# Layer 1's first convolution split twice and moved behind the projection, in a two-layer attention kernel

## The chip, the cores and the metric

The kernel runs on one core of one Trainium2 chip. The metric is the device time of one execution, in microseconds (us); the time of a kernel is the median of its runs. TensorE does the matrix products, VectorE (DVE) the two-input elementwise work, ScalarE (ACT) exponentials, copies and biases, GpSimd (POOL) a share of the elementwise work, and SyncE (SP) issues most of the transfers. Each engine executes its own queue in order.

## The reference

Eight images of 512 channels and 1024 pixels (32 x 32) in fp32 go through two attention layers. Cut to what matters:

```
# layer 0: 8 heads of 64 channels
h = group_norm(x, 32 groups)
q, k, v = split(w_qkv @ h + b_qkv)
weight = softmax(q_head^T k_head / 8)            # 1024 x 1024 for each head
x = x + w_proj @ (weight applied to v) + b_proj
# layer 1: one head of 512 channels
xn = group_norm(x, 8 groups)
q, k, v = q_w @ xn + q_b, k_w @ xn + k_b, v_w @ xn + v_b
attn = softmax(q^T k / sqrt(512))
x = x + p_w @ (attn applied to v) + p_b
```

## The kernel before

**Products merged ahead of time.** For layer 1 the kernel never forms q, k and v. It multiplies the weights once, in the prologue: m from the weights of q and k, and z from those of v and p. Then per image g = m h + ubias (the "first convolution" of the title, named g), scores = h^T g, and the values are read straight from z h.

**One level of Strassen.** Every large product goes through `wino` (L227): both factors are cut in two by two, and seven products take the place of eight. A product is a `step` (L240), 8 records of 128x512 on TensorE for a convolution. The sums of parts that it needs are made ahead of it: for weights by `left_sums` (L151), for images by `right_sums` (L165), eight subtractions of 128x512 (`image_factors`, L340). The order of steps is 1, then `middle`, then 4 and 3. The last two are not issued at once but laid in `tail`, and the next stage's `wino` issues them after its own step 1 (`finish`, L223), so that there is always a product between a stage's end and its readers. PSUM pools a, b and c have two buffers each; step 2 adds into the bank of step 1 after a copy of it (`t`, L249) has been taken, and steps 6, 7 and 4 share a bank.

**Two levels.** Layer 0's k and q of images 1 to 7 are split once more by `conv2` (L416): 49 products of 256 columns, in pairs `(1, 5), (2, 6), (7,), (3, 4)`. They need *inner factors* (L400), 28 subtractions of 128x256 on GpSimd per image, and twice-split weights that the prologue makes on GpSimd and writes to DRAM (`keep2`, L296, four operations of 128x896 and seven transfers). VectorE adds the products up (L439), GpSimd does the additions for the lone pair (`more`, L444), and four activations on ScalarE put the bias on, half a channel tile at a time (`biased_half`, L451).

**Order of the stages.** TensorE's instructions are pinned in program order (`matmul`, L66); the other engines' instructions are ordered by the framework unless they are pinned too (`tc.keep_in_program_order`). Small work is laid in `background`, from which each step takes a few, or in `hooks` of a stage's steps. The loop at L928 runs for each image b:

- layer 0's attention of image b (`attention0`, L577): 8 blocks (4 head pairs `hp`, 2 halves `tb`), each with 32 score products, exponentials of 128x1024 on ScalarE (L594), their running sum on VectorE (L596, L598), 32 products with v, and then the sums over keys on TensorE and the reciprocals (`reciprocals`, L548). The reciprocals go through DRAM (`rows`, `r`) to be spread over partitions; GpSimd multiplies the block by r (L615), and for the last block VectorE does (`scaled`, L617). Work for other stages goes in 16 slots, `extra`, two per block: group norm's application for layer 1 of image b-1 (`apply`, L140, ScalarE) stands in slots 3, 5, 7 and 9
- for b > 0, g of image b-1 (`layer1_scores`, L892), one-level, then the projection of image b (`projection`, L838) with its residual additions (L845, L847) and statistics (L98, L103), then layer 1's scores (`scores1`, L623: part 0 and part 1), z and values (`values1`, L672) of image b-1. Group norm's two small products for image b (`gmean`, `gvar`) stand in hooks of the scores' part 0
- v, k and q of image b+1 (`values`, `keys_and_queries`).

Weights come from DRAM through three buffers of 4 x 7 x 512 bytes per partition each (`wpool`), in the order of the list `uses` (L310 to L314), one `load_weight` (L317) per use. The prologue (L752) makes m, the factors of q, k and v, and image 0's v, q and k; the factors of p, m and z are made in image 0's attention (`later`, L797).

Of the kernel before, what the change touches and what calls it, by code (L numbers as in the profile page):

```python
# [29 lines left out]
def two_attention_blocks_kernel(  # L30
# [145 lines left out]
    def main_path(ctx):  # L176
# [117 lines left out]
        wdram2 = {n: dram.tile([P, 7, 7, P], F32, name=f"sums2_{n}") for n in "qk"}  # L294

        def keep2(n, t):  # L296

            u = wpool.tile([P, 4, 7, P], F32, tag="w", name=f"prepare2_{n}")
            quarter = lambda k, i: t[:, :, k, ts(i, P)]
            a11, a21, a12, a22 = quarter(0, 0), quarter(0, 1), quarter(1, 0), quarter(1, 1)  # L300
            s1, s2, s3, s4 = (u[:, i, :, :] for i in range(4))
            for dst, x, y, op in (
                (s1, a21, a22, ALU.add), (s2, s1, a11, ALU.subtract), (s3, a11, a21, ALU.subtract),
                (s4, a12, s2, ALU.subtract),
            ):
                nc.gpsimd.tensor_tensor(dst, x, y, op)
            for j, f in enumerate((a11, a12, s4, a22, s1, s2, s3)):
                nc.sync.dma_start(wdram2[n][:, :, j, :], f)

        twice = [("k", 0), ("k", 1), ("q", 0), ("q", 1)]  # L310
        uses = ["v", "p", *twice] if B > 1 else ["p"]
        for b in range(1, B):
            uses += ["m", "p", "z"] + (["v", *twice] if b + 1 < B else [])
# [3 lines left out]
        def load_weight():  # L317
            if uses:
                n = uses.pop(0)
                t = wpool.tile([P, 7 * C], F32, tag="w", name=f"w_{n[0]}_{len(uses)}")  # L320
                if n in twice:
                    t = t.rearrange("p (i j m) -> p i j m", i=4, j=7)
                    i = n[1]
                    t = t[:, : 4 - i]
                    nc.sync.dma_start(t, wdram2[n[0]][:, 4 * i : 4 + 3 * i])
                else:
                    t = t.rearrange("p (i k m) -> p i k m", i=7, k=2)
                    nc.sync.dma_start(t, wdram[n])
                loaded.append((n, t))
# [10 lines left out]
        def image_factors(h, uid):  # L340

            tiles = [pair_tile(f"t{i}_{uid}") for i in (1, 2, 4)]
            halves = lambda t: (t[:, :HT], t[:, HT:])
            return right_sums(
                [halves(t) for t in h[:2]], [halves(t) for t in h[2:]],
                [lambda j, t=t: t[:, j, :] for t in tiles], nc.vector.tensor_sub,
            )
# [52 lines left out]
        def inner_factors(hf, uid):  # L400

            f, steps = {}, []
            for p in ORDER:
                t = big_tile(f"inner{p}_{uid}", (P, 4, 2 * P))
                t1, t2, t3, t4 = (t[:, i, :] for i in range(4))
                b11, b12, b21, b22 = (hf[p][k][:, ts(i, 2 * P)] for k in range(2) for i in range(2))
                f[p] = {1: b11, 2: b21, 3: b22, 4: t4, 5: t1, 6: t2, 7: t3}

                def make(ops=((t1, b12, b11), (t2, b22, t1), (t3, b22, b12), (t4, b21, t2))):
                    for dst, x, y in ops:  # L410
                        nc.gpsimd.tensor_tensor(dst, x, y, ALU.subtract)

                steps.append(make)
            return f, steps

        def conv2(n, f, bias, name, hooks=(), late=None):  # L416
# [123 lines left out]
            last = [lambda: biased_half(0, 1), lambda: biased_half(1, 0)]  # L540
# [3 lines left out]
            pair(3, (3, 4), [(0, 1), (1, 0)], [(0, 1), (1, 0)], [load_weight, *last])  # L544
# [3 lines left out]
        def reciprocals(total, uid, across):  # L548
# [14 lines left out]
            nc.sync.dma_start(rows.rearrange("j i n -> i j n"), rc[0:P:32, :, :])  # L563
            if across:
                r = pair_tile(f"r_{uid}")
                for j in range(2):
                    row = rows[j : j + 1].rearrange("j i n -> j (i n)")
                    nc.sync.dma_start(r[:, j, :], row.to_broadcast([P, HT]))
            else:
                r = rpool.tile([P, HT], F32, tag="r", name=f"r_{uid}")  # L570
                for j in range(2):
                    row = rows[j : j + 1].rearrange("j i n -> j (i n)")
                    nc.sync.dma_start(r[ts(j, 64), :], row.to_broadcast([64, HT]))
# [3 lines left out]
        def attention0(b, q, k, v, extra):  # L577
            a = channel_tiles(f"a0_{b}")
            n = 0
            for hp in range(KC):  # L580
                for tb in range(2):
# [31 lines left out]
                    r = reciprocals(total, uid, False)  # L613
                    if (hp, tb) != (KC - 1, 1):
                        nc.gpsimd.tensor_tensor(dst, dst, r, ALU.mult)  # L615
                    else:
                        scaled = lambda dst=dst, r=r: nc.vector.tensor_mul(dst, dst, r)  # L617

            assert not extra
            return a, scaled  # L620


        def scores1(b, gf, hf, uid, hooks):  # L623
# [7 lines left out]
            def part(j):  # L631
# [34 lines left out]
                wino(f"sc_{uid}_{j}", mm, done, middle=(6, 2, 5, 7) if j else (2, 5, 6, 7), hooks=() if j else hooks)  # L666
# [85 lines left out]
        def prologue():  # L752
# [35 lines left out]
            k = conv(weight_factors(first["k"][0]), hf, pcols("bk0"), "k0_0")  # L788
            finish()
            keep2("k", first["k"][0])  # L790
# [7 lines left out]
            for n in "pmz":  # L798
                t, steps = prepare(n)
                later.append(steps)  # L800
                later.append([lambda n=n, t=t: keep(n, t), load_weight])
# [3 lines left out]
                lambda: tc.keep_in_program_order(nc.vector.tensor_add(obias[0], bias[2], pcols("bp0"))),  # L805
            ])
# [27 lines left out]
        def attention_steps(a, scaled, b):  # L834
            af, steps = image_factors(a, f"a_{b}")
            return af, [[], [scaled, lambda: background.extend(steps)]]

        def projection(b, af, xt):  # L838

            norm = GroupNorm(1, f"1_{b}")  # L840

            def residual(i, r, c, ps, u):
                oc = 2 * r + i
                xh = xt[oc][:, ts(c, HT)]
                nc.vector.scalar_tensor_tensor(xh, ps, obias[0][:, oc : oc + 1], xh, ALU.add, ALU.add)  # L845
                if u is not None:
                    nc.vector.tensor_add(xh, xh, u)  # L847
                background.append(lambda: norm.half_stats(oc, c, xh))

                if c == 1 - r:  # L850
                    background.append(lambda: norm.end_stats(oc))
# [6 lines left out]
            by_channel(weight("p"), af, f"p_{b}", residual, after=[load_weight, store])  # L858
            return norm

        def norm_hooks(norm, uid):
            return [
                [], [], [all_background], [lambda: norm.group_mean(acc_tile(f"gmean_{uid}")[:, :KC])],
# [3 lines left out]
        def values(b, h, hooks=()):  # L867

            hf, steps = image_factors(h, f"h0_{b}")
            background.extend(steps)  # L870
# [21 lines left out]
        def layer1_scores(b, h, hooks):  # L892
            hf, steps = image_factors(h, f"h1_{b}")
            background.extend(steps)
            g = conv(
                weight("m"), hf, ubias, f"g1_{b}", middle=(2, 5, 6, 7), hooks=hooks, back=4,
                after=[load_weight, lambda: background.extend(gsteps)],
            )
# [6 lines left out]
            return hf, gf  # L905

        def layer1_rest(b, hf, gf, hooks, ahead):
            e, total, ef = scores1(b, gf, hf, f"1_{b}", hooks)
            state = {}

            def sums():
# [3 lines left out]
                weight("z"), hf, f"z1_{b}", hooks=[[], [], [], [], [sums]], back=3,  # L915
# [12 lines left out]
        for b in range(B):  # L928
# [11 lines left out]
            for i, f in enumerate(applies):  # L940
                extra[2 * i + 3].append(f)
            if b > 0:
                extra[0] += late
            psum_pools(f"attention_{b}", 1)
            a, scaled = attention0(b, q, k, v, extra)
            psum_pools(f"products_{b}", 2)
            xt = [load_x(b, c, "x") for c in range(KC)]
            af, ends = attention_steps(a, scaled, b)
            if b > 0:
                hf, gf = layer1_scores(b - 1, h, ends)  # L950
                norm1 = projection(b, af, xt)
# [5 lines left out]
                layer1_rest(b - 1, hf, gf, norm_hooks(norm1, f"1_{b}"), ahead)  # L957
                if b + 1 < B:
                    v, f, norm0 = values(b + 1, h)
                    q, k, late = keys_and_queries(b + 1, f, norm0, ())  # L960
            elif B > 1:
                v, f, norm0 = values(1, h, ends)
                norm1 = projection(0, af, xt)
                q, k, late = keys_and_queries(1, f, norm0, norm_hooks(norm1, "1_0")[1:])
            else:
                for f in sum(ends, []):
                    f()
                all_background()
                norm1 = projection(0, af, xt)
                finish()  # L970
                for f in sum(norm_hooks(norm1, "1_0"), []):
# [4 lines left out]
        hf, gf = layer1_scores(B - 1, h, ())  # L976
        layer1_rest(B - 1, hf, gf, (), ())
# [196 lines left out]
```

## Time and profile before

| what | value |
|---|---|
| median of three runs | 2906.97 us (2901.96 to 2907.82) |
| profiled execution, its own time | 2902.66 us |
| its span | 2900.9 us |
| TensorE busy | 2886.5 us |
| VectorE busy | 1932.5 us |
| ScalarE busy | 872.2 us |
| GpSimd busy | 468.9 us |
| transfers | 267.97 MB, 92 GB/s on the mean |

How to read it: the profile is one execution, followed by the hardware. The page's first part gives each engine's busy time, its share of the span and its instructions. A timeline line has the start and duration of a run of like instructions in us, engine, line, operation, output<-inputs by the program's names, shape and count; in brackets is the idle time before it and who ended it. Ends of TensorE's products are modelled, so two lines overlap a little; distances of starts are the better measure. TensorE's lines all carry the line of the helper `matmul` (L67); the names of the tiles tell the stage (`psa_g`: pool a, stage g). An fp32 product is two records. A waits line says engine, what waited, what it waited for, total us, times, and the longest.

### The profile page before, as it was taken

The page shows a single profiled execution, that of the slowest core. Times are in us where ns is not written, and L with a number is a line of the kernel's source. Part 1 is how long each engine was busy: PE and PEld are TensorE (multiplying, and loading weights), DVE is VectorE, ACT ScalarE, POOL GpSimd, SP SyncE. Part 2 cuts the span into 40 slices and gives each one's busy share as a digit, 9 for nine tenths or more (in the row PEclk, how much of TensorE's full clock was granted, in tenths as well). Part 3 has the DMA queues.
Part 4 walks back from the last instruction along what each step waited for, and adds up shares of the span by engine and source line. Part 5 has one row for each costly group of instructions (what it writes and reads, how often), then busy time and mean ns, then how long its engine had stood idle before and what let it go on. Part 6 is the DMA issues. An engine that isn't in the chain of part 4 may idle for free.

```text
span 2900.9 us, 29024 instructions
## 1 busy us (share of the span) xinstructions
PE 2886.5 (100%) x10838; PEld 1500.3 (52%) x10838; DVE 1932.5 (67%) x2613; ACT 872.2 (30%) x1117; POOL 468.9 (16%) x525
## 2 busy tenths in 40 slices
PE   9999999999999999999999999999999999999999
PEld 5435634565345653457434574346733458334544
DVE  5488687567766578665776557866577665776555
ACT  1251451214512055121551115411163112631110
POOL 3023210032200321003210122102121031110000
PEclk9999999999999999999999999999999999999999
DMA  8433403123122231222212232122411224011201
GB/s 277 153 137 109 159 19 110 72 103 132 34 98 92 95 113 48 84 92 105 107 48 80 92 135 77 48 80 99 154 55 44 80 103 151 26 59 65 94 1 66
DMA packets 84186, 267.97 MB, mean 92 GB/s; under 512 B 10371, under 2 KB 29891, under 8 KB 75974
## 3 DMA queue, kind: packets, MB, share of 16 engines
q1 hardware_dynamic: 83622, 265.89, 25.5%
q8 instruction: 87, 1.43, 0.2%
q14 instruction: 61, 0.50, 0.1%
q10 hardware_dynamic: 416, 0.16, 0.0%
HBM read 216.30 MB, written 49.72 MB: 92 GB/s over the span
## 4 chain that ended last, share of the span: by engine, by line
PE 98%; issue 1%; DVE 0%; POOL 0%; ACT 0%; DVEq 0%; POOLq 0%
PE sc L67 16%; PE av L67 15%; PE psb_sc L67 6%; PE psb_av L67 6%; PE psa_av L67 4%; PE psa_sc L67 4%; PE psc_av L67 4%; PE psc_sc L67 4%; PE psb_g L67 3%; PE psb_z L67 3%; PE psb_p L67 3%; PE psb_v L67 3%; PE psb_k L67 3%; PE psb_q L67 2%; PE psa_g L67 2%; PE psa_v L67 2%
## 5 line engine op out<-in xcount | busy, mean ns | idle before, releaser
L598 DVE TENSOR_TENSOR sum<-sum,e 128x1024 f32<-128x1024 f32 x384 | 518.6, 1351 | 40.4 <-DVE sum L598 0.5
L594 ACT ACTIVATE e<-sc 128x1024 f32<-128x1024 f32 x512 | 476.8, 1052 | 72.9 <-PE sc L67 72.9
L67 PE MATMUL sc<-q,k 64*128 64x512 f32 x2048 | 458.3, 596 | 0.0
L67 PE MATMUL av<-e,v 128*64 128x512 f32 x2048 | 453.6, 595 | 0.0
L67 PEld LDWEIGHTS sc<-q,k 64*128 64x128 f32 x2048 | 192.3, 186 | 239.3 <-ACT e L594 110.3
L67 PEld LDWEIGHTS av<-e,v 128*64 128x64 f32 x2048 | 141.4, 137 | 304.3 <-issue 302.3
L561 POOL TENSOR_TENSOR all_recs<-all_recs,rc 128x256 f32<-128x256 f32 x72 | 64.4, 894 | 880.2 <-DVE rc L559 880.2
L559 DVE RECIPROCAL rc<-sums 128x256 f32<-128x256 f32 x72 | 126.4, 1756 | 89.7 <-PE sums L67 87.4
L615 POOL TENSOR_TENSOR a<-a,r 128x512 f32<-128x512 f32 x56 | 109.5, 1955 | 274.0 <-DMA r<-rows 247.5
L646 ACT ACTIVATE e<-e 128x512 f32<-128x512 f32 x96 | 60.5, 630 | 232.7 <-DVE e L645 232.7
L612 ACT COPY a<-av 128x512 f32<-128x512 f32 x64 | 37.4, 585 | 305.2 <-PE av L67 305.2
L596 DVE TENSOR_TENSOR sum<-e,e 128x1024 f32<-128x1024 f32 x64 | 78.6, 1228 | 59.8 <-ACT e L594 59.8
L67 PE MATMUL psa_sc<-g,h 128*128 128x512 f32 x256 | 115.7, 594 | 0.0
L67 PE MATMUL psa_av<-e,z 128*128 128x512 f32 x256 | 113.3, 595 | 0.0
L128 POOL TENSOR_TENSOR rstd<-ve,mhalf 128x4 f32<-128x4 f32 x16 | 16.7, 1043 | 499.9 <-DVE ve L126 499.9
L140 ACT ACTIVATE h<-h,b,s 128x1024 f32<-128x1024 f32 x62 | 78.5, 1270 | 60.7 <-DMA h<-in_x 48.0
L67 PEld LDWEIGHTS psa_sc<-g,h 128*128 128x128 f32 x256 | 48.1, 190 | 57.9 <-issue 56.2
L67 PEld LDWEIGHTS psa_av<-e,z 128*128 128x128 f32 x256 | 48.0, 190 | 57.3 <-issue 55.4
L67 PE MATMUL psb_k<-inner_h,w_k 128*128 128x256 f32 x294 | 75.4, 383 | 0.0
L67 PE MATMUL psb_q<-inner_h,w_q 128*128 128x256 f32 x294 | 74.9, 383 | 0.0
L249 ACT COPY t_sc<-psa_sc 128x512 f32<-128x512 f32 x32 | 18.7, 585 | 181.7 <-DVE x L847 152.4
L444 POOL TENSOR_TENSOR k<-k,k 128x256 f32<-128x256 f32 x28 | 20.0, 727 | 291.0 <-DVE u_k L439 291.0
(304 smaller groups left out, 4580.8 us busy)
## 6 DMA issues: line engine op xcount, KB each, us to landing
x<-in_x SPq DMA_DIRECT2D x36, 512.0 KB
h<-in_x SPq DMA_DIRECT2D x32, 512.0 KB
r<-rows SPq DMA_DIRECT2D x128, 128.0 KB
spill<-x SPq DMA_DIRECT2D x32, 512.0 KB
h<-spill SPq DMA_DIRECT2D x32, 512.0 KB
x<-spill SPq DMA_DIRECT2D x32, 512.0 KB
out<-x SPq DMA_DIRECT2D x64, 256.0 KB
w_p<-sums_p SPq DMA_DIRECT2D x8, 1792.0 KB
```

The source lines that it names most:

```text
L67: tc.keep_in_program_order(nc.tensor.matmul(*args, **kw))
L140: tc.keep_in_program_order(nc.scalar.activation(dst, src, AF.Identity, bias=b, scale=s))
L249: nc.scalar.copy(t1[i], ps["a", i])
L444: nc.gpsimd.tensor_tensor(d, x, y, ALU.add)
L559: nc.vector.reciprocal(rc, sums)
L561: nc.gpsimd.tensor_tensor(all_recs, all_recs, rc, ALU.add)
L594: nc.scalar.activation(e, sc, AF.Exp, scale=(C // 8) ** -0.5)
L596: nc.vector.tensor_add(total, es[0], e)
L598: nc.vector.tensor_add(total, total, e)
L612: nc.scalar.copy(dst, av)
L615: nc.gpsimd.tensor_tensor(dst, dst, r, ALU.mult)
L646: nc.scalar.activation(dst, dst, AF.Exp, scale=scale)
```

## The change

- In the stage of images b = 1 to 7 the projection of image b comes first, and g of image b-1 after it. g goes through `conv2("m", ...)`; only image 7's own g, behind the loop, stays one-level. After g, `finish()` issues its last products before the scores begin.
- h1's image factors (eight subtractions) are put in the slots of layer 0's attention on VectorE, and h1's application moves from slots 3, 5, 7, 9 to 1, 3, 5, 7. The inner factors of h1, 28 subtractions, follow on GpSimd after the attention, pinned. The image factors of `a` are pinned on VectorE, four in the attention's slots, three after it, one in the projection's third hook behind `scaled`. In image 0's stage h0 of image 1 takes the place of h1.
- The last head pair's blocks run in the order 1, 0, and the transfers of the last block's rows and r are issued by ScalarE's queue.
- The projection's middle order is 5, 6, 7, 2 in place of 6, 2, 5, 7. One of its residual additions comes a step later (`add_rest`). Its statistics are gathered and laid in the background of the scores' part 0; `gmean` moves to the scores' part 1, and `gvar` (norm's second product) to z, a stage later each.
- The prologue makes the twice-split factors of m too (`prepare("m")` beside k, `keep2("m")` behind it); `keep2("k")` moves ahead of the convolution k. m is loaded in two parts (1792 and 1344 KB) in place of one of 1792 KB.

The diff, cut to its core:

```diff
-        wdram2 = {n: dram.tile([P, 7, 7, P], F32, name=f"sums2_{n}") for n in "qk"}
+        wdram2 = {n: dram.tile([P, 7, 7, P], F32, name=f"sums2_{n}") for n in "qkm"}
...
-            uses += ["m", "p", "z"] + (["v", *twice] if b + 1 < B else [])
+            uses += ["p", *twice["m"], "z"] + (["v", *twice["k"], *twice["q"]] if b + 1 < B else [])
...
-                        nc.gpsimd.tensor_tensor(dst, x, y, ALU.subtract)
+                        pin(nc.gpsimd.tensor_tensor(dst, x, y, ALU.subtract))
...
-            last = [lambda: biased_half(0, 1), lambda: biased_half(1, 0)]
+            last = [lambda: biased_half(1, 0), lambda: biased_half(0, 1)]
...
-            pair(3, (3, 4), [(0, 1), (1, 0)], [(0, 1), (1, 0)], [load_weight, *last])
+            pair(3, (3, 4), [(0, 1), (1, 0)], [(0, 1), (1, 0)], [load_weight, *last, *after])
...
-                for tb in range(2):
+                for tb in (0, 1) if hp < KC - 1 else (1, 0):
...
-                    r = reciprocals(total, uid, False)
-                    if (hp, tb) != (KC - 1, 1):
+                    last = (hp, tb) == (KC - 1, 0)
+                    r = reciprocals(total, uid, False, nc.scalar if last else nc.sync)
+                    if not last:
...
-            k = conv(weight_factors(first["k"][0]), hf, pcols("bk0"), "k0_0")
+            keep2("k", first["k"][0])
+            t, steps = prepare("m")
+            k = conv(weight_factors(first["k"][0]), hf, pcols("bk0"), "k0_0", hooks=[[], [], [], [], steps])
             finish()
-            keep2("k", first["k"][0])
+            keep("m", t)
+            keep2("m", t)
...
-                background.append(lambda: norm.half_stats(oc, c, xh))
+                stats.append(lambda: norm.half_stats(oc, c, xh))
...
+            by_channel(
+                weight("p"), af, f"p_{b}", residual, middle=(5, 6, 7, 2), hooks=[[], [], hooks, [], [add_rest]],
+                after=[load_weight, store],
+            )
+            return norm, stats
...
-            g = conv(
-                weight("m"), hf, ubias, f"g1_{b}", middle=(2, 5, 6, 7), hooks=hooks, back=4,
-                after=[load_weight, lambda: background.extend(gsteps)],
-            )
+            after = [lambda: background.extend(gsteps)]
+            if inner:
+                g = conv2("m", inner, ubias, f"g1_{b}", after=after)
+            else:
+                g = conv(weight("m"), hf, ubias, f"g1_{b}", middle=(2, 5, 6, 7), back=4, after=[load_weight, *after])
...
-                extra[2 * i + 3].append(f)
+                extra[2 * i + 1].append(f)
...
+                hf, t = image_factors(h, f"h1_{b - 1}")
                 extra[0] += late
+                for i, fs in enumerate((t[:1], t[1:2], (t[2], t[4]), (t[6], t[3]), (t[5], t[7]), steps[:2], steps[2:4])):
+                    extra[2 * i + 3] += fs
...
-                hf, gf = layer1_scores(b - 1, h, ends)
-                norm1 = projection(b, af, xt)
+                inner, sums2 = inner_factors(hf, f"h1_{b - 1}", tc.keep_in_program_order)
+                for f in sums2:
+                    f()
+                norm1, stats = projection(b, af, xt, [scaled, steps[7]])
+                gf = layer1_scores(b - 1, hf, inner)
...
-                layer1_rest(b - 1, hf, gf, norm_hooks(norm1, f"1_{b}"), ahead)
+                _, *means, affine = norm_hooks(norm1, f"1_{b}")
+                hooks = [[], [], [lambda: background.extend(stats)]], [[], [], *means], affine
+                layer1_rest(b - 1, hf, gf, hooks, ahead)
```

## The prediction

> **What bounds the kernel now.** I read the page's first part (busy time by engine), then its chain, then the answer on TensorE's waits.
>
> ```profile
> PE 2886.5 (100%) x10838; PEld 1500.3 (52%) x10838; DVE 1932.5 (67%) x2613; ACT 872.2 (30%) x1117; POOL 468.9 (16%) x525
> ...
> PE 98%; issue 1%; DVE 0%; POOL 0%; ACT 0%; DVEq 0%; POOLq 0%
> ```
>
> ```profile
> PE tr_wk L70 <- DMA rawk<-in_w: 4.0, 2, 3.8
> PE psa_v L67 <- POOL h L142: 0.8, 1, 0.8
> PE psb_v L67 <- DVE w_v L238: 0.5, 1, 0.5
> ```
>
> TensorE is busy for 2886.5 of 2900.9 us, the chain that ends last is 98% TensorE, and all its waits together are about 7 us (4.0 of them the first weights' load). So the time is the sum of TensorE's own work. Work taken from it shows in full, and every new wait of TensorE shows in full.
>
> The timeline of TensorE gives the prices. First image 1's g as it is now, interleaved with the projection:
>
> ```profile
> 1165.13 3.60 PE L67 MATMUL psc_g<-t_h,w_m 128*128 128x512 f32 x8
> 1168.56 3.60 PE L67 MATMUL psb_g<-t_h,w_m 128*128 128x512 f32 x8
> 1172.00 3.60 PE L67 MATMUL psb_g<-h,w_m 128*128 128x512 f32 x8
> 1175.43 3.60 PE L67 MATMUL psa_p<-a,w_p 128*128 128x512 f32 x8
> ```
>
> The starts are 3.43 us apart: that is a step of a one-level convolution (seven steps, 24.03 us). Then q of the next image, which is already split twice, with its last stretch:
>
> ```profile
> 1019.27 1.03 PE L67 MATMUL psb_q<-inner_h,w_q 128*128 128x256 f32 x4
> 1020.13 0.59 PE L67 MATMUL psa_q<-h,w_q 128*128 128x256 f32 x2
> 1020.56 0.59 PE L67 MATMUL psa_q<-t_h,w_q 128*128 128x256 f32 x2
> ...
> 1038.78 0.70 PE L67 MATMUL psc_q<-h,w_q 128*128 128x256 f32 x2
> 1039.32 0.59 PE L67 MATMUL psc_q<-t_h,w_q 128*128 128x256 f32 x2
> 1039.75 1.03 PE L67 MATMUL psb_q<-inner_h,w_q 128*128 128x256 f32 x4
> 1040.70 0.70 PE L67 MATMUL sc<-q,k 64*128 64x512 f32 x2
> ```
>
> One small product takes 0.4315 us (1020.13 to 1020.56), and there are 49.
>
> Last, one block of layer 0's attention (14.65 us each), VectorE and then TensorE:
>
> ```profile
> 1133.39 8.76 DVE L598 TENSOR_TENSOR sum<-sum,e 128x1024 f32<-128x1024 f32 x6
> 1143.70 1.76 DVE L559 RECIPROCAL rc<-sums 128x256 f32<-128x256 f32 x1 [1.55 <-PE sums L67]
> ```
>
> ```profile
> 1135.92 7.09 PE L67 MATMUL av<-e,v 128*64 128x512 f32 x32
> 1142.94 0.64 PE L67 MATMUL sums<-sum,ones 128*32 128x256 f32 x8
> ```
>
> VectorE's last addition ends at 1142.15, and TensorE takes the sum at 1142.94: 0.79 us to spare.
>
> **What the Trainium skill says.** "TensorE: Matmul & The Clock Gate", Step-by-step, says that throughput is "purely N cycles" of the columns streamed. The trace agrees: 3.43/8 = 0.429 us for a record of 512 columns, 0.4315/2 = 0.216 for one of 256; small products carry no surcharge. "VectorE: DVE Perf Modes", the errata section, prices an fp32 tensor_tensor at (N+151)/0.96 ns: 0.69 us for 512, 1.22 for 1024; the trace has 0.68 and 1.23. "SBUF — State Buffer", two separate sides, says that a VectorE operation with two SBUF inputs and a GpSimd one lock each other out. The trace agrees: GpSimd's inner subtractions (L411) take 0.72 us beside a quiet VectorE and 1.14 to 1.8 where VectorE subtracts in SBUF. "DMA: Bandwidth & Descriptors", Issuing engines are not separate DMA queues, says that another issuing engine saves only the issue time; nothing here shows otherwise, so I give the move of the last r to ScalarE's queue no gain.
>
> **The change, part by part.** T is the end of an attention, E the end of g, in an image's stage.
>
> 1. *g split twice, 7 of 8 times.* Removed: 24.03 us each. Added: 49 x 0.4315 = 21.14, and the gaps. q from 1016.68 to 1040.70 is 24.02, less k's tail in it (1.73) and the two little norm products with their hitch (0.46): 21.83. g's tail now runs uncovered ahead of the scores just as q's does ahead of the attention, so I take 21.83. Gain 2.20 x 7 = 15.4 us. This is not in dispute: 28,672 columns become 25,088.
>
> 2. *ScalarE at E.* conv2 ends with four bias activations (L451, 0.68 apart), queued ahead of the copy t_sc of the scores' first product. They are released by TensorE's last product and its additions, so the copy is done at about E+3.6; the scores' step 2 writes over that bank and is ready at E+3.43. Wait 0.2 to 0.4 us an image; I take 0.25: +1.75. In the trace before the projection's tail stood there and hid it.
>
> 3. *h1's eight subtractions and a's first four on VectorE inside the attention.* A block leaves VectorE 1.55 us after the last addition and 0.79 before it. In the built order most land after the last addition (no cost). One alone before it is 0.69, inside 0.79. In one block of each of images 1 to 7 two stand before it: 1.25 to 1.4 less 0.79 is 0.45 to 0.6 us; I take 0.46: +3.2 (to 4.2). In image 0's attention three blocks have two: +1.35 (to 1.8). Bound below zero: none, TensorE has no wait here now.
>
> 4. *The projection first.* Its middle order 5, 6, 7, 2 puts `scaled` (L617) in its third step's hook. r of the last block: recip ends T+2.0, rows and r take some 6 us more (1145.48 to 1151.14 in another block), so it lands near T+8; the first product that needs it is at T+13.7. Cover 5 us: nothing. ScalarE is held at the r DMAs from T+2 to about T+4, and the copy t_p queues behind; its reader comes at T+8.6. Nothing. The last a*r on GpSimd is now the block before, ready before T. x's loads are issued at T-10 to T-7 and needed at T+13.7. In image 1's stage the values step takes psc first, whose VectorE evacuation stands behind norm statistics of the image ahead: +1.0 once (0 to 3).
>
> 5. *The inner factors of h1: 28 subtractions on GpSimd.* 23.3 us now (163.3/7 by the rows of L411). They begin at T+3.4, the first pair is wanted at T+24.9 (done near T+10), the last at T+38 (done near T+27). Cover 11 to 15 us; no cost. Per pair, conv2's other additions (L439, L444) are those of q, which TensorE didn't wait for except once for 0.4.
>
> 6. *Statistics and g's sums moved into the scores.* Twelve statistics operations (8 x 0.68 + 4 x 0.2 = 6.2) and the eight 512-wide sums of g (5.5), which stood under the projection, now come after E. VectorE is busy 27.2 of the 48.5 us from 1209.76 to 1258.30; with them about 37. Walking the built order with these prices, VectorE has the w factors of part 1's step 7 ready at E+43.5 and E+44.3, and TensorE wants the bank at E+44.8: 0.5 to 1.3 us to spare. I take nothing, but this is the thinnest cover that repeats.
>
> 7. *Prologue and weights.* keep2 of m adds four GpSimd operations of 2.08 us and 5 MB of writes, at 97 to 115 us, where the DMA engines move 0 to 11 GB/s; its loads are issued at 81 and land by 87, before VectorE wants them at 94.5. m's weights come in parts of 1792 and 1344 KB in place of 1792, two uses ahead, at a mean of 92 GB/s. 0 +- 0.5.
>
> Sum: -15.4 + 1.75 + 3.2 + 1.35 + 1.0 = -8.1 us; with the ends of each term -12.5 to -4. The profiled execution of before took 2902.66 us (span 2900.9 and 1.8 around it), so the like one after is 2894.6. The three runs' median lies 4.3 above the profiled one; on that footing 2906.97 - 8.1 = **2898.9 us**.
>
> **Rivals.**
> - *A: the stalls of 2 and 3 don't come* (chance 0.22): the subtractions slip behind the sums, or ScalarE is fast enough. For it: my places rest on half-microseconds. Against: the order in a queue is fixed. -15.4 + 1 to 2, so about 2893.
> - *B: VectorE falls behind in the scores* (0.18): the cover of 6 is used up. Price: each microsecond past it costs 7. The forecast has 8.1/7 = 1.16 us an image to lose; from about 1.2 + 0.9 = 2.1 us of extra lateness at E+44 it ends slower than before, and at 3 us it gives 2906.97 - 8.1 + 7 x (3 - 0.9) = 2913.6. For it: VectorE loses to GpSimd's lock, and e's activations on ScalarE may come later behind biases. Against: GpSimd is nearly empty there, one 1.56 us copy (L650).
> - *C: it doesn't pay as it says* (0.2): other waits of a few tenths at each change of stage (the g pairs' banks, the projection's tail, `scaled`) take 0.6 to 1.2 us an image more. Then 2903 to 2907, no change. The trace before has such hitches: 0.2 and 0.1 in q's tail, 0.4 once.
>
> My own case has 0.40.
>
> **Numbers.** The measurement tells a change from none at about 0.2%, 5.8 us. Faster than 2901.2: mine 0.36, A 0.22, C 0.02: 0.60. Within: 0.04 + C 0.17 + B 0.03: 0.24. Slower: B 0.15 + C 0.01: 0.16. The range runs from A's full gain, 2906.97 - 15.4 = 2891.6, taken at 2891, to the mild half of B, 2909.
>
> **What would show it.** g's records at 256 columns with starts 0.43 apart and 21.8 us from first to last, TensorE records up by 7 x (98 - 56) = 294; TensorE waits `psa_sc` for ScalarE at about 0.25 x 7, `sums` for VectorE at 0.45 once an image and three times in image 0. The inner factors' wait should be absent. I am wrong if `psb_sc` or `psa_g` waits appear seven times at over 1 us, if `psa_p` waits for `a`, or if TensorE's busy time falls by less than 15.

## The result, and the profile after

| | before | after |
|---|---|---|
| median of four runs | 2906.89 us (2901.96 to 2907.82) | 2902.51 us (2901.33 to 2902.90) |
| ratio after/before, 95% interval | | 0.9988 (0.9970 to 1.0005) |
| span of the profiled execution | 2900.9 us | 2899.5 us |
| TensorE busy | 2886.5 us, 10838 records | 2876.1 us, 11132 records |

The interval takes in 1: no difference is shown. Most executions of the kernel before lie near 2902 or near 2907, in every set of runs; the profiled one is of the lower kind, and the changed kernel's four all lie near 2902. Profile against profile, the change gains 1.3 us (2902.66 against 2901.33). Below I compare variants with the changed kernel (2902.51, span 2899.5), since the median of before moves by 4 us from set to set.

TensorE has 294 records more and is 10.4 us less busy, so the split takes work from it. But TensorE waits longer. The page's first part and the answer on TensorE's waits, of the changed kernel:

```profile
PE 2876.1 (99%) x11132; PEld 1556.2 (54%) x11132; DVE 2004.1 (69%) x2753; ACT 922.4 (32%) x1201; POOL 703.8 (24%) x781
```

```profile
PE ps_wz L67 <- issue: 4.4, 1, 4.4
PE tr_wk L70 <- DMA rawk<-in_w: 3.7, 1, 3.7
PE psb_v L67 <- DVE u_v L238: 3.6, 1, 3.6
...
PE sums L67 <- DVE sum L598: 0.2, 1, 0.2
```

Beside the first weights' load, which TensorE waited for before too (4.0 us), two waits stand out, and each occurs once. That of 4.4 us (0.5 before) is in the prologue, ahead of z's product; that of 3.6 us is new, in image 0's stage, in the values of image 1. To find where the time went I took the starts of TensorE's `sums` products, 72 marks through the run, in both traces, and compared the stretches between them:

| stretch | after less before |
|---|---|
| prologue, up to the first block's sums (141.03 against 134.32) | +6.71 |
| image 0's attention | +0.64 |
| image 1's v, image 0's projection, image 1's k and q | +4.14 |
| seven stages with projection, g, scores, z | -14.03 (-1.95 in five, -2.06 and -2.20 in two) |
| seven attentions of images 1 to 7 | +1.47 (0.21 each) |
| everything else | -0.38 |
| sum | -1.45 |

The stretch behind the last mark adds 0.12. So the part that repeats gains 12.6 us net, and 10.9 us are lost in two places that come once. In the stages themselves the small products of g, two records each, start 0.43 us apart, as in q. The prediction took its lines of g from about 1165 us and calls it image 1's; by the count of the attentions this stage has the projection of image 3 and the g of image 2, and the prices are the same. Behind that g the changed kernel's timeline of TensorE has the scores' first steps:

```profile
1212.14 7.23 PE L67 MATMUL psa_sc<-g,h 128*128 128x512 f32 x16
1219.20 3.60 PE L67 MATMUL psc_sc<-sg,t_h 128*128 128x512 f32 x8
```

The first two steps (16 records) take 1219.20 - 1212.14 = 7.06 us in place of 2 x 3.43 = 6.87: that is the wait of 0.19 us behind ScalarE's biases. In the last experiment but one, with g one-level in the same order, the two steps take 6.87 us.

Now the prologue. Timeline of all engines around the wait, changed kernel (a line in which several like instructions are joined gives their joint duration):

```profile
97.53 8.30 POOL L306 TENSOR_TENSOR prepare_m<-prepare_m 128x896 f32<-128x896 f32 x4 [23.89 <-DVE prepare_m L286]
...
100.59 1.21 DVE L117 TENSOR_TENSOR d<-mv,gmean 128x4 f32<-128x4 f32 x1
101.83 2.00 DVE L119 TENSOR_TENSOR d<-d 128x4 f32<-128x4 f32 x1
...
103.86 1.99 DVE L121 TENSOR_TENSOR dv<-d,mv 128x4 f32<-128x4 f32 x1
105.78 1.27 DVE L718 COPY natv<-tr_wv 128x512 f32<-128x512 f32 x2
...
106.56 6.08 PE L67 MATMUL ps_wz<-rawp,natv 128*128 128x512 f32 x7 [4.38 <-issue]
```

The same operations before, and z's product before:

```profile
100.78 0.16 DVE L119 TENSOR_TENSOR d<-d 128x4 f32<-128x4 f32 x1
100.97 0.16 DVE L121 TENSOR_TENSOR dv<-d,mv 128x4 f32<-128x4 f32 x1
101.88 1.29 DVE L716 COPY natv<-tr_wv 128x512 f32<-128x512 f32 x2 [0.75 <-PE tr_wv L70]
...
102.68 13.97 PE L67 MATMUL ps_wz<-rawp,natv 128*128 128x512 f32 x32 [0.50 <-ACT natv L716]
```

Three operations on four columns take 1.21, 2.00 and 1.99 us instead of 0.16. They end at 101.8, 103.8 and 105.9, where the second, third and fourth of GpSimd's new operations (four of 2.08 us from 97.53) end too. Behind them in VectorE's queue stand the copies of wv's transposes, and TensorE needs those for z's product: it starts at 106.56 in place of 102.68. That is 3.9 of the 6.7 us. The rest is the clock; columns of this view are stretch, its length, busy us of TensorE, weight loads, VectorE, ScalarE and GpSimd, then the granted clock (1.00 is full speed), the busy share of the DMA engines and their GB/s:

```profile
106.00:113.00 7.00, 6.44 (x9) 2.78 (x10) 1.05 (x2) 0.00 (x0) 0.00 (x0) 0.55 0.81 242
113.00:124.00 11.00, 11.00 (x33) 4.85 (x34) 0.16 (x1) 2.34 (x4) 0.24 (x1) 1.00 0.64 199
```

After the idle 4.4 us TensorE runs at about half clock to 113; z's product takes 123.20 - 106.56 = 16.64 us from its start to the next product's, instead of 13.80: the other 2.8 us.

In image 0's stage the trace of the changed kernel shows, on VectorE and on GpSimd:

```profile
258.00 5.60 DVE L960 TENSOR_TENSOR t_a<-a 128x512 f32<-128x512 f32 x2
263.53 0.68 DVE L238 TENSOR_TENSOR u_v<-psb_v,t_v 128x512 f32<-128x512 f32 x1
```

```profile
259.16 0.73 POOL L411 TENSOR_TENSOR inner_h<-h,inner_h 128x256 f32<-128x256 f32 x1
259.85 1.41 POOL L411 TENSOR_TENSOR inner_h<-t_h 128x256 f32<-128x256 f32 x2
261.21 1.85 POOL L411 TENSOR_TENSOR inner_h<-t_h,inner_h 128x256 f32<-128x256 f32 x2
```

The first t_a (L960, two inputs in SBUF) takes 4.48 us, the second 1.20, beside GpSimd's row of subtractions; the evacuation u_v, which TensorE waits for, stands behind both. The row has no gap until 261.93; there is one of 0.08 us ahead of its last operation, and the first t_a ends at 262.48, right behind it. So it is in all four kernels that keep t_a in this place.

**Theory**: the repeating gain is the split's; what ate it is the lock between GpSimd and VectorE's operations with two SBUF inputs (the one that the prediction cites), in two places where a PSUM evacuation that TensorE waits for stands behind such an operation. **Rivals**: the prologue has too much work or traffic (the additional subtractions, 5 MB of writes); in image 0's stage the order of the steps or the norm statistics are late, as my step 4 said; the new order takes or gives a part of the stage's 2 us.

### The profile page after: what moved, and what is told of

The parts are those of the page before. It is cut to its first block, busy times and chain, and to the rows that moved or that the text cites. A ratio compares the mean times of both kernels' runs of the same rounds, so it can differ in the third digit from the quotient of the medians.

```text
span 2899.5 us, 30282 instructions
## 1 busy us (share of the span) xinstructions
PE 2876.1 (99%) x11132; PEld 1556.2 (54%) x11132; DVE 2004.1 (69%) x2753; ACT 922.4 (32%) x1201; POOL 703.8 (24%) x781
## 3 DMA queue, kind: packets, MB, share of 16 engines
q10 hardware_dynamic: 1792, 2.29, 0.2%
q8 instruction: 90, 1.47, 0.2%
## 5 line engine op out<-in xcount | busy, mean ns | idle before, releaser
L128 POOL TENSOR_TENSOR rstd<-ve,mhalf 128x4 f32<-128x4 f32 x16 | 36.2, 2261 | 267.8 <-DVE ve L126 267.8
L411 POOL TENSOR_TENSOR inner_h<-h,inner_h 128x256 f32<-128x256 f32 x112 | 95.6, 856 | 2.7
L411 POOL TENSOR_TENSOR inner_h<-h 128x256 f32<-128x256 f32 x56 | 57.0, 1019 | 151.3 <-PE psc_av L67 151.3
L652 POOL COPY sum<-e 128x1024 f32<-128x1024 f32 x8 | 8.8, 1101 | 283.6 <-ACT e L648 283.6
```

The lines of the kernel that those rows point to most:

```text
L128: nc.gpsimd.tensor_tensor(rstd, ve, mhalf, ALU.pow)
L411: pin(nc.gpsimd.tensor_tensor(dst, x, y, ALU.subtract))
```

## The experiments

**m's factors later.** Edit to the changed kernel:

```diff
-            k = conv(weight_factors(first["k"][0]), hf, pcols("bk0"), "k0_0", hooks=[[], [], [], [], steps])
+            k = conv(weight_factors(first["k"][0]), hf, pcols("bk0"), "k0_0")
             finish()
-            keep("m", t)
-            keep2("m", t)
...
             wv = natural(raw_v, "v", "bc")
+            for f in steps:
+                f()
+            keep("m", t)
+            keep2("m", t)
```

> The changed kernel with one move in the prologue: the four VectorE subtractions of m's factors and keep2 of m (four GpSimd operations of 2.08 us and the writes) come behind the copies of wv's transposes. Theory ([...]VectorE's three tiny norm operations with two SBUF inputs wait a whole 2.08 us operation each): they take 0.16 us each again, TensorE's wait of 4.4 us ahead of ps_wz shrinks to about 0.5, the following products keep the full clock, and the first sums come 6.7 us earlier, near 134.3 us; in all some 6.7 us less than the changed kernel, about 2896. Rival (the additional VectorE subtractions or m's writes as such are too much for the prologue): the work is only shifted, VectorE or the DMA engines are late for z's product or the first attention instead, and less than half of the 6.7 us comes back.

2900.62 us (2898.24 to 2902.44), span 2900.7. The first half of the theory came true: the tiny operations take 0.16 us, ps_wz waits 0.5 us, the first sums stand at 133.92, 7.1 us earlier. But the rival's sentence came true as well: image 0's attention lost 6.3 us of it, 5.1 of them between its first two marks, and image 0's stage 1.5 more. By the medians 1.9 us came back; this profile's span is even 1.1 us longer than the changed kernel's. SyncE's and ScalarE's timelines of this kernel:

```profile
117.82 1.39 SPq L308 DMA_DIRECT2D sums_m<-prepare_m  x1
...
130.82 2.15 SPq L209 DMA_DIRECT2D h<-in_x  x4
```

```profile
137.73 1.24 ACT L140 ACTIVATE h<-h,b,s 128x1024 f32<-128x1024 f32 x1 [9.22 <-DMA h<-in_x]
```

m's writes wait on SyncE's queue for GpSimd, and the loads of h behind them are issued at 130.8 (the first of them at 125.9 in the changed kernel). The application of h, which the change put in the first block's slot and which is pinned on ScalarE, waits for its load to 137.7 with the next block's exponentials behind it. The move put writes that wait in front of loads that the next stage needs. That is read from the trace; no run moves the loads alone.

**The copies on ScalarE** (act_copies). m's factors stay where they are:

```diff
-        def natural(wt, nm, banks):
+        def natural(wt, nm, banks, copies=None):
...
-            spread(lambda o, copy: tc.keep_in_program_order(copy(t[o], pt[o])), KC)
+            spread(lambda o, copy: tc.keep_in_program_order((copies or copy)(t[o], pt[o])), KC)
...
-            wv = natural(raw_v, "v", "bc")
+            wv = natural(raw_v, "v", "bc", nc.scalar.copy)
```

> The changed kernel with keep2 of m left where it is, but all four copies of wv's transposes on ScalarE in place of two on VectorE. Theory (VectorE locked out by GpSimd): VectorE's tiny norm operations still take 1.2 to 2.0 us each, since GpSimd's operations still run beside them, but TensorE no longer waits for VectorE there; its wait ahead of ps_wz falls from 4.4 to some 0.5 to 2 us, the clock stays up, and 4.5 to 6 us come back. Rival (DMA traffic or a late input): the copies or ps_wz are late on ScalarE too, and the wait stays above 3 us.

2896.70 us (2894.43 to 2898.91), span 2893.7. VectorE's timeline of this kernel, then TensorE's:

```profile
101.04 2.00 DVE L119 TENSOR_TENSOR d<-d 128x4 f32<-128x4 f32 x1
103.08 2.00 DVE L121 TENSOR_TENSOR dv<-d,mv 128x4 f32<-128x4 f32 x1
```

```profile
101.73 14.00 PE L67 MATMUL ps_wz<-rawp,natv 128*128 128x512 f32 x32 [0.35 <-ACT natv L718]
```

GpSimd, the traffic and VectorE's delay are all unchanged, and TensorE neither waits nor slows down. That rules out the traffic, and says that only the copies behind the delay counted. The first sums stand at 133.40, 7.6 us earlier (0.8 of them lie ahead of this place: GpSimd's four operations begin at 96.75, not 97.53); 1.5 were given back in image 0's stage, where this time TensorE ran at half clock after the wait for u_v (the eight records behind it took 3.67 us, 1.99 in the changed kernel).

**One operand in PSUM.** GpSimd, queue and order unchanged; one of the three tiny operations reads its second input from PSUM:

```diff
-            nc.vector.tensor_sub(d, mean, self.gmean)
+            nc.vector.tensor_sub(d, mean, ps)
```

> The changed kernel with one operand of one operation changed: the norm's d = mean - gmean reads gmean from PSUM, not its SBUF copy, everywhere; same values. GpSimd's 2.08 us operations in the prologue stay. Theory (only VectorE operations with two SBUF inputs wait for GpSimd): this operation takes about 0.16 us in place of 1.21, the next one (d*d) then waits for the running GpSimd operation, and dv for the one after it, so VectorE is through one GpSimd operation earlier: the wait ahead of ps_wz falls from 4.4 to about 2.4 us. Rival (VectorE is slowed by GpSimd or the DMA traffic in general): the operation still takes over 1 us and the wait stays at 4.4.

2895.64 us (2893.41 to 2899.50), span 2897.7. GpSimd's and VectorE's timelines of this kernel:

```profile
97.10 8.31 POOL L306 TENSOR_TENSOR prepare_m<-prepare_m 128x896 f32<-128x896 f32 x4 [23.92 <-DVE prepare_m L286]
...
100.03 0.15 DVE L117 TENSOR_TENSOR d<-mv,gmean 128x4 f32<-128x4 f32 x1
100.21 1.16 DVE L119 TENSOR_TENSOR d<-d 128x4 f32<-128x4 f32 x1
101.40 1.99 DVE L121 TENSOR_TENSOR dv<-d,mv 128x4 f32<-128x4 f32 x1
103.31 1.27 DVE L718 COPY natv<-tr_wv 128x512 f32<-128x512 f32 x2
```

The operation with one SBUF input takes 0.15 us while GpSimd runs; the next one with two takes the wait over. TensorE's wait is 2.36 us. Both as the theory said to a tenth, so in the prologue the second SBUF input is the cause, and not load in general. The kernel's times spread more than others', and the profiled execution is the longest of the five: by its span 1.8 us came back, by the medians 6.9. Half-clock stretches after the two waits left (z's product 15.5 us, the eight records behind u_v 3.49) are what the trace shows; what the shorter executions do there is not traced.

**a's factors behind v** (a_after_v). In image 0's stage:

```diff
-                v, f, norm0 = values(1, hf, [[], steps[:2], steps[2:4], steps[4:6], [steps[6], scaled, steps[7]]])
+                v, f, norm0 = values(1, hf, [[], [], [], [], [*steps[:7], scaled, steps[7]]])
```

> The changed kernel with one move in image 0's stage: the image factors of a come on VectorE behind the evacuations of v's last own step, not between them. Theory (the pinned subtraction t_a of 4.5 us waits for GpSimd's row of inner factors, and the evacuation u_v behind it is late): t_a takes about 0.7 us each, TensorE's wait psb_v for u_v (3.6 us) is gone, the stage is some 4 us shorter, about 2898.5. Rival (the order psc first in the projection or the norm statistics of the image ahead are late, as the prediction had it): the wait only moves to psb_v for w_v or to psc_p, and at most 1 to 2 us come back.

2896.84 us (2896.13 to 2897.35), span 2895.1, 4.4 less. The wait for u_v is gone and none took its place:

```profile
258.86 0.67 DVE L238 TENSOR_TENSOR u_v<-psb_v,t_v 128x512 f32<-128x512 f32 x1
...
264.43 1.29 DVE L960 TENSOR_TENSOR t_a<-a 128x512 f32<-128x512 f32 x2
```

The norm statistics of the image ahead still stand between the evacuations and delay nobody; so my step 4's mechanism was not the one. t_a now runs when GpSimd is through, and two of them take 1.29 us together. So the place of t_a in VectorE's queue is shown as the cause of the wait; that GpSimd's row made it long is read from the traces, since no run takes the row away.

**Both moves of the first and fourth experiments** (both_moves).

> The changed kernel with both moves (m's twice-split factors behind the copies, a's image factors behind v's evacuations). Theory: the two costs are independent, so 6.7 + 4 = some 10.7 us come back and the time is about 2892, 0.5% under the kernel before; what is left is 14 us gained in seven stages less some 2 us of waits at the sums. Rival (the costs hide one another, or the time lost is of another kind): less than 7 us come back.

2895.23 us (2894.05 to 2896.30), span 2893.7: 7.3 us came back, not 10.7. The missing part is the one that the first experiment had already lost in image 0's first blocks (the exponentials behind the late h: TensorE waits 2.0 us for e and 1.4 for a sum). The two costs do not hide one another; the first repair was a poor one.

**The two good repairs together**: act_copies and a_after_v in one kernel (copies_and_a).

> The changed kernel with the two moves that came off: all copies of wv's transposes on ScalarE, and a's image factors behind v's evacuations in image 0's stage. Theory (two independent places where VectorE is locked out or late): act_copies gave 5.8 us and a_after_v 5.7, together 10 to 11.5; about 2891.5, 0.4% under the kernel before, with the spans' ledger showing the first sums near 133.4 us and no wait of TensorE over 1 us beyond the first weights'. Rival (both recover the same time, as in both_moves, where 7.3 came back in all): about 2896.

2890.21 us (2890.02 to 2890.52), span 2888.2; ratio to the kernel before 0.9951 (0.9937 to 0.9964). It is faster than both kernels. 12.3 us came back of the changed kernel's time (11.3 by the spans), and TensorE waits nowhere over 1 us except for the first weights.

**One-level g in that kernel**, everything else kept; the seven g's twice-split product and the inner factors of h1 are left out, so that the same result is computed with one level less:

```diff
-            uses += ["p", *twice["m"], "z"] + (["v", *twice["k"], *twice["q"]] if b + 1 < B else [])
+            uses += ["p", "m", "z"] + (["v", *twice["k"], *twice["q"]] if b + 1 < B else [])
...
-                g = conv2("m", inner, ubias, f"g1_{b}", after=after)
+                g = conv(weight("m"), hf, ubias, f"g1_{b}", middle=(2, 5, 6, 7), back=4, after=[load_weight, *after])
...
-                inner, sums2 = inner_factors(hf, f"h1_{b - 1}", tc.keep_in_program_order)
-                for f in sums2:
-                    f()
+                inner = True
```

> copies_and_a with g one-level again (m loaded in one part, no inner factors of h1), everything else of the change kept: the projection first, h1's factors in the attention, the moved statistics. Theory (the gain is the split alone, 2.0 us an image as the stages' ledger says): 14 us more than copies_and_a. Rival (a part of the stage's gain comes from the new order, or the order costs something that the split hides): clearly less, or more, than 14.

2903.91 us (2903.51 to 2905.03): 13.7 us more, 1.96 a stage. The stage of image 1 takes 114.61 us between its marks, exactly as in the kernel before (112.66 with the split), and so do four more of the seven; two are 0.35 and 0.17 shorter, where the kernel before has a hitch. So in the stages the split gains nearly all. The new order has a price elsewhere: with or without the split the attentions are 2.5 us longer than in the kernel before, for the subtractions put in them, and the span without it, 2901.9, is 1.0 longer.

**The sums.** In copies_and_a, VectorE's order in the attention written out, with the two subtractions of a slot behind the reciprocals:

```diff
-                            nc.vector.tensor_add(total, total, e)
+                            tc.keep_in_program_order(nc.vector.tensor_add(total, total, e))
...
-            nc.vector.reciprocal(rc, sums)
...
+            pin = (lambda ins: ins) if across else tc.keep_in_program_order
+            pin(nc.vector.reciprocal(rc, sums))
...
                     r = reciprocals(total, uid, False, nc.scalar if last else nc.sync)
+                    for f in subs.pop(0) if subs else ():
+                        f()
...
-                    extra[2 * i + 3] += fs
+                    subs[i + 1] += fs
```

> copies_and_a with the order of VectorE in layer 0's attention written out: sums, reciprocals and h1's (in image 0's stage h0's) image factors pinned, the two subtractions of a slot standing right behind the reciprocals of their block, not ahead of the last addition. Theory (the 0.2 us that TensorE waits for a sum, three times in image 0 and once in each later image, comes from two subtractions ahead of the last addition; behind the reciprocals they are 1.4 us late by at most 0.6, which the 0.79 us to spare takes in): all those waits go, 0.2 x 10 and one of 0.5 = about 2.3 us less than copies_and_a, about 2888. Rival (the delay is only moved: the first addition starts later and the last one ends as late): the waits stay or come in more blocks, same or slower than copies_and_a.

2894.04 us (2893.95 to 2895.61), 3.8 more: a miss, the rival is right. The one wait of 0.21 us became four of 0.12 an image (14.77 us between sums for 14.65), one of 1.1 came up in image 0, and small ones in g and q. VectorE's timeline of one block, from behind the reciprocals:

```profile
760.58 1.81 DVE L967 TENSOR_TENSOR t_h<-h,t_h 128x512 f32<-128x512 f32 x2
762.32 1.21 DVE L597 TENSOR_TENSOR sum<-e,e 128x1024 f32<-128x1024 f32 x1
763.63 8.76 DVE L599 TENSOR_TENSOR sum<-sum,e 128x1024 f32<-128x1024 f32 x6
```

The two take 1.81 us here, not 1.4: the first takes 1.21, beside GpSimd's addition to all_recs (0.90 us from 760.35). The additions behind them, each of which needs the one ahead, have no slack among themselves: what they start late they end late.

## Why the prediction held in its range, and which steps of it failed

The forecast was 2898.9 and the time is 2902.51: inside the range, and the median fell as forecast, by 4.4 us in place of 8.1. That it fits so well is luck. The forecast put the new median 4.3 us above a profiled execution because the old one lay so; the new one lies 1.2 above (2902.51 over 2901.33). Profile against profile the forecast was -8.1 and the result -1.3: steps 4 and 7 cost 9.8 us more than forecast; step 3, priced too high, and small differences elsewhere gave some 3 back. (The ends that its terms state add up to -3.1 at the upper end, not -4, and to -14.5 at the lower if step 3 costs nothing.) One of its own signs of being wrong came: TensorE's busy time fell by 10.4 us, less than 15. Of the 4.6 us that are missing, 2.8 are z's product at half clock; in the kernel with both good repairs, which has no such stretch, it falls by 14.4, to 2872.1, still a little short. By its steps:

1. *g split twice*: right. From g's first record to the scores' first are 28.75 us, less the 6.87 of the projection's two steps in it: 21.88, for 21.83 forecast. With the wait of step 2 the gain is 1.95 a stage, as forecast; one-level g behind the projection costs 1.96 more.
2. *ScalarE at E*: right, 0.19 for 0.25.
3. *Subtractions inside the attention*: right place and mechanism, size too large. One wait each in images 1 to 7, 0.21 for 0.46; three in image 0, 0.64 in all for 1.35. I charged the two their full 1.28 us, but they put the last addition only 1.02 us later: it starts at 413.37 in image 1's block, where without them it would be 412.35, since each addition otherwise starts 0.10 us behind the end of the one ahead and the subtractions run without that pause. 1.02 less the 0.79 to spare is 0.23. I also missed what the spare had already paid for. Of the six additions in the block that the prediction shows, five take 1.23 us and one 2.11, beside GpSimd's multiplication by r (1.98 us from 1136.43). If that is the same lock, as the times suggest, it costs 0.88 us in such a block, more than the whole wait; no run moves the multiplication.
4. *The projection first*: the cover of `scaled`, of x and of the ScalarE queue held. The term "+1.0 once (0 to 3)" failed: 4.1, and by another mechanism. I had put the late evacuation down to norm statistics; it was late behind t_a, which took 4.48 us beside GpSimd's row.
5. *Inner factors of h1*: right, no wait for them.
6. *Statistics and g's sums in the scores*: right, no wait of `psb_sc`; rival B did not come.
7. *Prologue*: failed, and it is the largest error: "0 +- 0.5" was 6.7. I checked that the writes fit the idle traffic (idle to 110 us; from there to 115 the engines move 108 GB/s, which I had overlooked) and that VectorE gets its inputs in time. I did not ask what the four additional GpSimd operations do to VectorE beside them, although the prediction itself cites "SBUF — State Buffer", two separate sides, for exactly this lock, and applies it to GpSimd's side only. The trace agrees with that page in both directions: GpSimd's operations went from 0.72 to 1.8 us, and VectorE's from 0.16 to 2.0. The prediction's bound was also too narrow for want of the clock: 2.8 of the 6.7 us are TensorE at half speed after the wait.

The page "TensorE: Matmul & The Clock Gate", Why this matters for your kernels, warns of idle gaps over about 3 us between bursts. The clock fell to about 0.55 after a wait of 4.4 us, which agrees. But z's product took 15.5 us for 13.8 after a wait of 2.4 us, and after one of 3.6 us in the changed kernel the clock did not fall (1.00 from 264 to 266 us), so in these traces the length of TensorE's wait alone does not decide it.

Rival C gave about the right time for a wrong reason: the small waits at every change of stage did not come.

What stays open: why t_a lost five turns in a row to GpSimd in image 0's stage, while before the change one beside the same row took 1.29 us; and why the clock falls after one wait and not after another like it. Ahead of the wait in the prologue TensorE has only transposes (16 of them, from 99.67 us) and one small product, ahead of the other it has products; whether that matters no run shows.

## What to carry to other kernels

Work added to GpSimd "in idle time" isn't free if VectorE runs operations with two SBUF inputs beside it: here one of 0.16 us took 2.0, as long as the GpSimd operation beside it (2.08). So look for what stands behind it in VectorE's queue, above all PSUM evacuations that TensorE waits for. Two cures were tried. Giving the evacuation to ScalarE took TensorE's wait from 4.4 to 0.35 us; letting one operand of the first of three such operations come from PSUM took it to 2.36. And a ledger of marks that both traces share tells in one table whether a gain was never there or was given back elsewhere.

## What the runs showed of the hardware that was not expected

- A wait of TensorE can be charged twice: 4.4 us idle cost 2.8 us more at about half clock (0.55 from 106 to 113 us). It need not be: after 3.6 us idle in image 0's stage the next eight records took 1.99 us in the changed kernel and 3.67 with the copies on ScalarE.
- A subtraction of 128x512 on VectorE took 4.48 us beside a gapless row of GpSimd operations of 0.7 us each, so the loser does not always get its turn at the next boundary between them.
